# Loads of delta * x written six units ahead instead of seven, later planned landings, and two tiles in turn, in a four-layer scan, edge and attention kernel

## The chip, the cores and the metric

The kernel runs on one core of one Trainium2 chip. The metric is the device time of one execution in microseconds (us), as the median of three runs. An execution agrees with the others to within 2.3 us (14132.37 to 14134.62).

## The reference, cut to what matters

The input x has shape (4, 64, 64, 128): four images of 4096 places with 128 channels. Four layers follow each other. Layers 0 and 1 hold a selective scan, and they are where the change lies. Layer 2 gates nine neighbours of each place; layer 3 is attention over 7 x 7 neighbourhoods. Both run after the scans and are not touched.

Layer 0 splits the channels in two halves of 64. The left half passes two 3 x 3 convolutions; the right half is projected to 128 channels, passes a 3 x 3 depthwise convolution and the scan. Layer 1 normalizes its input, projects it to 256 channels twice (one half is convolved depthwise and scanned, the other is a gate), and adds a two-layer perceptron afterwards. In both, the scan goes over the 4096 places in four directions k (rows, columns, and both backwards), for each channel d and 16 states n:

```
delta = softplus(dt)                           # dt, B, C: projections of x
h[d,n] = exp(delta[d] * A[d,n]) * h[d,n] + (delta[d] * x[d]) * B[n]
y[d]   = sum over n of h[d,n] * C[n]
```

The four directions' y are added, with a skip term D * x.

## The kernel before, in words

**The scans.** A task is 128 channels of one image: 4 tasks in layer 0, 8 in layer 1 (two per image). A task has 16 steps, which are 4 directions by 4 pieces of 1024 places. A step has 16 units; a unit is 8 channels by 16 states on the 128 partitions, over 1024 places. So there are 12 x 16 x 16 = 3072 units. `Scans.run` (from line 556) is a loop over units u. In slot u it writes out, for each engine, work of several units:

- SP (SyncE) issues all transfers. `load(u + 7)` (lines 614 and 615, body from 422) brings delta * x of one unit from DRAM into a tile dub of 512 KB, repeated over the 16 states. Dub has five buffers (line 427), so a load waits until POOL has read the load five before. What it reads, dud, is written per step by one transfer at line 394. The first load of a step (g == 0) first flushes all waiting transfers of the preparation (lines 424 and 425).
- POOL (GpSimd) multiplies dub by B for unit u + 3 (`times_b`, line 436) into one half of a pair tile h, of which there are three.
- PE (TensorE) spreads delta over partitions for unit u + 2 (line 444), from a tile dp that twelve transfers of 64 KB bring per step (line 405), and ACT (ScalarE) takes exp of delta * A (line 446, tile da).
- DVE (VectorE) runs the scan of unit u (line 455) and, for each pair of units, multiplies h by C (line 465). PE then adds over the states (line 536) and ACT copies results and end states (lines 476, 482, 546).

**Preparation and side work.** Beside this loop two lanes of other work are dealt out in small pieces. The lane "prep" (`prepare`, from 317) makes one step's delta, dud, dp and the repeated B and C: it projects x on PE, copies the result to xd (ACT), stores xd to DRAM (`store_xd`, lines 346 to 351), and goes on from there. It starts 22 units before its step, in slots u with (u + 22) % 16 == 0 (lines 582 to 595); in that same slot the last step's leftovers are flushed ("prep" and "rep", line 586). The lane "side" runs the other parts of layers 0 and 1 for other images: `pre0` (projections before the scan, 888), `depthwise` (778), `convs` (925) with `conv` (815), `post0` (955), `pre1` (1000: norm and projection of layer 1), `post1` (1035). These lanes yield, after each piece, the engine that their next piece needs, and may add a time before which it should not be written.

**What sets the order.** No scheduler moves instructions. `Plan` (line 114) keeps an estimate of when each engine is done, in us, with a unit counted as UNIT = 3.6. `Lane.fits` (182) lets a piece be written into the current slot if the estimate says that it is done in time. Three constants say how long after its issue a transfer is taken to have landed: LANDING (8.0 us, most transfers, line 109), FOUR_LANDING (12.0, four loads at once in `post1`, line 110), ROWS_LANDING (17.0, the padded rows of the convolutions, line 111). They are used when a lane waits for a load (`fetch` 740, `halves` 766, `prepare` 320 and 356) and when a tile that is being stored should be free again (`store` 712, `when` 724). Stores and preparation transfers are not issued where they are written: `post` (137) puts them in a list with the estimated time of their data, and `flush` (144) issues those that are due at the beginning of a slot. So between two dub loads on SP stands the group of transfers that became due, or were written directly, in one slot.

**Tiles of the side lane.** `Side.tile` (695) has one buffer each for the tags d0, d1, sq, o and x2 (128 x 512, 256 KB), and two for x and pad. In `pre1` (lines 1018 to 1024) the two projections m = 0 and 1 of a chunk go through sq to DRAM (xid), and the norm of the next chunk writes sq again (line 863). In `convs` (936 to 947) each result of the first convolution goes through d0 to DRAM (ld); `conv` yields a plain "ACT" for it (line 839), with no regard to the store before. ACT's write into such a tile waits until the earlier store has read it. Instructions written through `Counted` (74) all carry line 97.

Of the kernel before, what the change touches and what calls it, by code (L numbers as in the profile page):

```python
# [18 lines left out]
H = 64  # L19
# [86 lines left out]
UNIT = 3.6  # L106
USUAL = dict(PE=1.4, ACT=0.7, TAB=3.3, POOL=1.3)
SLACK = dict(PE=1.2, ACT=2.2, POOL=3.0)
LANDING = 8.0
FOUR_LANDING = 12.0  # L110
ROWS_LANDING = 17.0


class Plan:
# [154 lines left out]
class Scans:  # L269
# [286 lines left out]
    def run(self, between):  # L556

        total = NU * len(self.tasks)
        first = self.tasks[0]
        first.W.load()  # L560
        for _ in self.fetch(first):
            pass
        for _ in self.prepare(first, 0):
            pass
        self.plan.start()
        pieces, fetch, fetched = Lane(self.plan, "prep", iter(())), iter(()), 0
        for u in range(-7, total):
            if u >= 0:
                self.scan(u)
            if 0 <= u + 3 < total:  # L570
                self.times_b(u + 3)
            if u >= 0 and u % NG == 0:
                self.bring_c(u)
            if u > 0 and u % 2 == 0:
                self.save(u // 2 - 1)
            if 0 <= u + 2 < total:
                self.decay(u + 2)
            if u > 0 and u % 2 == 0:
                self.add_up(u // 2 - 1)
            if u > 0 and u % 8 == 0:  # L580
                self.keep(u - 1)
            if u > 0 and u % 8 == 1:
                self.sum_so_far(u - 1)
            even, eighth, first_one = u % 2 == 0, u % 8 == 1, u % NG == 0
            self.plan.slot(
                u, 1.6 * even + 1.0 * eighth, 0.25 * even + 0.7 * (u % 8 == 0) + 1.1 * first_one
            )
            ahead, rest = divmod(u + AHEAD, NG)
            if rest == 0:
                while pieces.step():  # L590
                    pass
                self.plan.flush("prep", "rep")
            if rest == 0 and 0 < ahead < total // NG:
                n, step = divmod(ahead, NU // NG)
                if step == 0 and self.tasks[n].W is not self.tasks[n - 1].W:
                    self.tasks[n].W.load()
                if step == 0 and fetched < n:
                    fetch, fetched = self.fetch(self.tasks[n]), n
                    for _ in range(self.tasks[n].W.nct):
                        next(fetch, None)  # L600
                pieces = Lane(self.plan, "prep", self.prepare(self.tasks[n], step))

            n, step = divmod(ahead + 1, NU // NG)
            if step == 0 and fetched < n < len(self.tasks) and self.tasks[n - 1].x_done:
                fetch, fetched = self.fetch(self.tasks[n]), n
            next(fetch, None)
            while (pieces.count < rest - 4 or pieces.fits()) and pieces.step():
                pass
            if u >= 0:
                n, i = divmod(u, NU)  # L610
                if self.later:
                    self.later.pop(0)()
                between(n, i)
            if 0 <= u + 7 < total:
                self.load(u + 7)
        self.add_up(total // 2 - 1)
        self.save(total // 2 - 1)
        self.keep(total - 1)
        while self.later:
            self.later.pop(0)()  # L620


class Side:
# [191 lines left out]
    def conv(self, w, src):  # L815


        lo, hi = slice(0, H), slice(H, P)
        yield "SP"
        self.flush()  # L820

        def load(pad, half):
            self.rows(pad, hi, src, half * HW // 2 - 1, HW // 2 + 2)
            self.rows(pad, lo, src, half * HW // 2, HW // 2)

        tiles, start = self.halves(load)
        for c in range(0, NCH, 2):
            if c % 4 == 0:
                pad, landed = tiles.pop()
                if c == 0:  # L830
                    start(1)
            yield "PE", landed
            ps = self.bank()
            for t, (dy, dx) in enumerate(((0, 1), (0, 0), (0, 2), (2, 0), (2, 1), (2, 2))):
                part = hi if dy else slice(0, P)
                for j, half in enumerate((lo, hi)):
                    row = (c % 4 + j) * ROWS + dy
                    self.tap(ps[half, :], w[part, dx + 3 * (dy > 0), :], pad[part], row, dx, start=t == 0, stop=t == 5)
                yield "PE" if t < 5 else "ACT"
            yield c, ps  # L840

    def centered(self, xs, i):
# [45 lines left out]
    def pre0(self, b):  # L888

        self.before = True  # L890
        nc = self.nc
        wt = self.weights(self.d0a[:, 0 : 3 * P])
        cv12, inp = wt[:, 0:P], wt[0:H, P : 3 * P]
        lo, hi = slice(0, H), slice(H, P)
        x = self.fetch("x", self.x0[b, :, chunk(0)])
        for c in range(NCH):
            yield ("PE", self.landed) if c == 0 else "PE"
            ps = self.bank()
            nc.tensor.matmul(ps, cv12, x, start=True, stop=True)
            if c + 1 < NCH:  # L900
                x = self.fetch("x", self.x0[b, :, chunk(c + 1)])
            yield self.when("TAB", "d0")

            rl = self.tile("d0")
            self.act(rl, ps, AF.Silu, scale=self.cv12g, bias=self.cv12b)
            yield "PE POOL"
            l = self.tile("sq")
            nc.gpsimd.tensor_scalar(l[hi], rl[hi], self.bn0g[hi], self.bn0b[hi], ALU.mult, ALU.add)
            ps = self.bank()
            nc.tensor.matmul(ps, inp[:, 0:P], rl[lo], start=True, stop=True)  # L910
            yield self.when("ACT", "d1")
            xi = self.tile("d1")
            nc.scalar.copy(xi, ps)
            self.store("d1", self.xid[0, b, 0][:, chunk(c)], xi)
            self.store("sq", self.ld[b][0][:, chunk(c)], l[hi])
            yield "PE"
            ps = self.bank()
            nc.tensor.matmul(ps, inp[:, P : 2 * P], rl[lo], start=True, stop=True)
            yield self.when("TAB", "o")
            sz = self.tile("o")  # L920
            self.act(sz, ps, AF.Silu)
            self.store("o", self.szd[0, b, 0][:, chunk(c)], sz)
        yield from self.depthwise(self.dww0, self.dwb0, self.xid[0, b, 0], self.xcd[0, b, 0])

    def convs(self, b):

        self.before = True
        nc = self.nc
        yield "SP"
        wt = self.weights(self.d0a[:, 3 * P :])  # L930
        c3, cw = wt[:, 0:H], wt[:, H:].rearrange("p (n t c) -> p n t c", n=2, t=6)
        lo, hi = slice(0, H), slice(H, P)
        for i in range(2):
            for item in self.conv(cw[:, i], self.ld[b][i]):
                if isinstance(item, str) or isinstance(item[0], str):
                    yield item
                    continue
                c, ps = item
                l = self.tile("d0")
                nc.scalar.activation(l, ps, AF.Relu, scale=self.bn12g[i], bias=self.cb[:, i : i + 1])  # L940
                if i == 0:
                    self.store("d0", self.across(self.ld[b][1], 0, H, c), l)
                    yield "PE"
                    continue
                yield "PE"
                ps = self.bank()
                for half in (lo, hi):
                    nc.tensor.matmul(ps[half, :], c3[half], l[half], start=True, stop=True)
                yield self.when("ACT", "o")
                o = self.tile("o")  # L950
                nc.scalar.activation(o, ps, AF.Relu, bias=self.c3b)
                self.store("o", self.across(self.catd[b], 0, H, c), o)
                yield "PE"

    def post0(self, b):
# [3 lines left out]
        wt = self.weights(self.d0b)  # L959
        cv, outp, cv3 = wt[lo, 0:H], wt[:, H : 2 * H], wt[:, P : 2 * P]  # L960
        y = self.fetch("x", self.yd[0, b, 0][:, chunk(0)])
        yield "PE", self.landed
        for c in range(NCH):
            ns = []
            sz = self.tile("x2")
# [34 lines left out]
    def pre1(self, b):  # L1000
# [1 line left out]
        nc = self.nc  # L1002
        inp = self.weights(self.w1a)
        x = self.fetch("x", self.x1[b, :, chunk(0)])
        yield "PE", self.landed

        def project(m, xn):
            ps = self.bank()
# [3 lines left out]
        for c in range(NCH):  # L1012
# [4 lines left out]
                x = self.fetch("x", self.x1[b, :, chunk(c + 1)])  # L1017
            for m in range(2):
                ps = project(m, xn)
                yield self.when("ACT", "sq")  # L1020
                xi = self.tile("sq")
                nc.scalar.activation(xi, ps, AF.Identity, bias=self.bias1[:, m : m + 1])
                self.store("sq", self.xid[1, b, m][:, chunk(c)], xi)
                yield "PE"
            for m in range(2, 4):
                ps = project(m, xn)
# [1005 lines left out]
```

## Time and profile before

| what | value |
|---|---|
| median of 3 runs | 14134.09 us |
| lowest and highest run | 14132.37, 14134.62 us |
| profiled execution, its own time | 14152.81 us |
| its span, first to last instruction | 14151.0 us |
| DVE busy | 12084.3 us (85%) |
| PE, POOL, ACT busy | 10247.9 (72%), 9862.8 (70%), 8111.5 us (57%) |
| DMA: share of 16 engines, bytes | 73.3%, 2559.53 MB |
| granted TensorE clock, mean | 0.737 |
| scans: first dub load issued, last one read | 193.3 us, 11474.0 us |
| one scan of a unit (line 455), one product with C for two units (line 465), one product with B (line 436) | 2339, 2288, 2357 ns |

How to read it: the scans fill the first four fifths of the span, layers 2 and 3 the rest. DVE, PE, ACT and POOL execute; SP only issues transfers ("SPq") and is never counted busy. A waits row "A L1 <- B L2: total, times, longest" gives idle time of engine A just before instructions of its line L1, put down to what ended it: an instruction of engine B, or, after "DMA", the landing of a transfer "to<-from". For SP it is the time from its last instruction to the release of the next. A timeline row gives the start, the length, the engine, the line, the operation, the tiles, the number of merged instructions, and in brackets the idle time before it.

### The profile page before, as it was taken

The page shows a single profiled execution, that of the slowest core. Times are in us where ns is not written, and L with a number is a line of the kernel's source. Part 1 is how long each engine was busy: PE and PEld are TensorE (multiplying, and loading weights), DVE is VectorE, ACT ScalarE, POOL GpSimd, SP SyncE. Part 2 cuts the span into 40 slices and gives each one's busy share as a digit, 9 for nine tenths or more (in the row PEclk, how much of TensorE's full clock was granted, in tenths as well). Part 3 has the DMA queues.
Part 4 walks back from the last instruction along what each step waited for, and adds up shares of the span by engine and source line. Part 5 has one row for each costly group of instructions (what it writes and reads, how often), then busy time and mean ns, then how long its engine had stood idle before and what let it go on. Part 6 is the DMA issues. An engine that isn't in the chain of part 4 may idle for free. (4 is left out here: it accounts for less than half of the span.)

```text
span 14151.0 us, 120242 instructions
## 1 busy us (share of the span) xinstructions
PE 10247.9 (72%) x36408; PEld 2607.7 (18%) x36408; DVE 12084.3 (85%) x6647; ACT 8111.5 (57%) x10782; POOL 9862.8 (70%) x4606
## 2 busy tenths in 40 slices
PE   5777777777766777677776777777776766657999
PEld 1111111111111111111111111111111111113555
DVE  4899899989998899889998999999999945775666
ACT  3666566655665566556665555555555556654555
POOL 4777788778877788778887888888888853550000
PEclk7666767777677766677667777767777768878999
DMA  6888888888889888988889888888888842442000
GB/s 163 217 217 226 211 215 224 212 222 209 218 220 209 209 215 208 219 205 219 220 213 223 221 205 210 203 204 218 201 207 201 202 113 68 102 107 66 13 14 8
DMA packets 900351, 2567.23 MB, mean 181 GB/s; under 512 B 145271, under 2 KB 166911, under 8 KB 891511
## 3 DMA queue, kind: packets, MB, share of 16 engines
q1 hardware_dynamic: 899703, 2559.53, 73.3%
q8 instruction: 291, 4.77, 0.2%
q14 instruction: 357, 2.92, 0.1%
HBM read 2135.67 MB, written 272.37 MB: 170 GB/s over the span
## 5 line engine op out<-in xcount | busy, mean ns | idle before, releaser
L436 POOL TENSOR_TENSOR h<-dub,repB 128x1024 f32<-128x1024 f32 x3072 | 7173.7, 2357 | 1146.2 <-DMA dub<-dud 771.1
L455 DVE TENSOR_TENSOR_SCAN h<-da,state,h 128x1024 f32<-128x1024 f32 x2304 | 5324.0, 2339 | 492.2 <-ACT da L446 236.6
L446 ACT ACTIVATE da<-da,av 128x1024 f32<-128x1024 f32 x3072 | 3338.5, 1088 | 2906.8 <-PE da L444 2887.5
L444 PE MATMUL da<-dp,spread 96*128 96x512 bf16 x6144 | 2529.8, 505 | 2399.8 <-DVE h L455 2329.0
L465 DVE TENSOR_TENSOR hc<-h,C 128x2048 f32<-128x2048 f32 x1536 | 3513.6, 2288 | 139.4 <-ACT C L482 80.3
L536 PE MATMUL yps<-hc,gather 128*32 128x512 f32 x12288 | 2470.9, 889 | 5.6 <-DVE hc L465 5.6
L455 DVE TENSOR_TENSOR_SCAN h<-da,h 128x1024 f32<-128x1024 f32 x768 | 1729.7, 2279 | 373.3 <-POOL h L436 283.7
L444 PEld LDWEIGHTS <-spread 96*128 96x128 bf16 x6144 | 563.3, 108 | 5697.2 <-issue 5518.7
L97 POOL TENSOR_TENSOR delta<-delta,low 128x1024 f32<-128x1024 f32 x192 | 452.0, 2354 | 768.0 <-ACT low L97 648.3
L97 PE MATMUL ms<-d,wts 128*128 128x512 f32 (+3 forms) x900 | 691.5, 891 | 237.4 <-POOL d L97 119.9
L97 ACT ACT_TABLE_LOAD x600 | 769.8, 1283 | 12.4 <-PE ms L97 1.8
L97 PE MATMUL ms<-xd,xpdt 8*128 8x512 f32 (+1 forms) x768 | 630.2, 912 | 130.8 <-ACT xd L97 38.0
L97 ACT CAST parts<-delta 128x1024 bf16<-128x1024 f32 x384 | 400.6, 1043 | 363.2 <-POOL delta L97 348.9
L519 PE MATMUL yps<-y,ident 128*128 128x512 f32 x576 | 506.4, 969 | 94.9 <-ACT y L546 94.3
L97 ACT ACTIVATE low<-ms,av 128x512 f32<-128x512 f32 x384 | 263.9, 687 | 529.5 <-PE ms L97 523.9
L97 PE MATMUL ms<-pad,diag 96*32 96x504 f32 (+1 forms) x2304 | 404.6, 809 | 180.9 <-DMA pad<-xid 155.1
L1811 ACT ACTIVATE s<-s,nmax 128x512 f32<-128x512 f32 x512 | 366.1, 717 | 249.9 <-DVE nmax L1808 245.0
L97 POOL TENSOR_TENSOR low<-delta,xc 128x1024 f32<-128x1024 f32 x192 | 501.9, 2614 | 1.6
L1439 ACT ACTIVATE hid<-hid,relb 128x1024 f32<-128x1024 f32 x288 | 323.0, 1146 | 258.5 <-DVE hid L1434 258.4
L536 PEld LDWEIGHTS yps<-hc,gather 128*32 128x32 f32 x12288 | 283.8, 128 | 1012.7 <-issue 1004.5
L1541 POOL TENSOR_TENSOR acc<-acc,part 128x1024 f32<-128x1024 f32 x120 | 314.2, 2625 | 213.3 <-DVE part L1535 158.8
L1800 PE MATMUL sps<-k,q 32*128 32x512 f32 x1024 | 440.7, 658 | 21.2 <-DVE s L1807 21.2
(275 smaller groups left out, 11286.6 us busy)
## 6 DMA issues: line engine op xcount, KB each, us to landing
dub<-dud SPq DMA_DIRECT2D x3072, 512.0 KB
dp<-parts SPq DMA_DIRECT2D x2304, 64.0 KB
repB<-xdd SPq DMA_DIRECT2D x192, 512.0 KB
repC<-xdd SPq DMA_DIRECT2D x192, 512.0 KB
dud<-low SPq DMA_DIRECT2D x192, 512.0 KB
spread<-gd SPq DMA_DIRECT2D x72, 1024.0 KB
pad<-xid SPq DMA_DIRECT2D x192, 256.0 KB
szd<-o SPq DMA_DIRECT2D x96, 256.0 KB
```

The source lines that it names most:

```text
L97: return call(*args, **kw)
L436: self.nc.gpsimd.tensor_mul(dbu, self.live.pop(("dub", u)), t.prepared[step]["B"])
L444: self.nc.tensor.matmul(da[:, cols], self.C.spread[:, jj, :], dp[:, j, cols], start=True, stop=True)
L446: self.nc.scalar.activation(da, da, AF.Exp, scale=t.W.a[:, at : at + 1])
L455: nc.vector.tensor_tensor_scan(h[:, way], da[:, way], h[:, way], 0.0 if step % NSTEP == 0 else t.states[step - 1][:, u % NG : u % NG + 1], ...
L465: nc.vector.tensor_mul(hc, pair, t.prepared[step]["C"].unsqueeze(1).to_broadcast([P, 2, TS]))
L519: self.nc.tensor.matmul(self.like_part(yps, k), self.C.ident, self.part(t.y, k, c, b), start=True, stop=False)
L536: self.nc.tensor.matmul(out, self.C.gather[jj], rhs, start=False, stop=jj == 3)
L1439: nc.scalar.activation(hid, hid, AF.Gelu, bias=self.relb[:, m, t : t + 1])
L1541: (nc.vector if alone and pair else nc.gpsimd).tensor_add(acc, acc, part)
L1800: nc.tensor.matmul(sps[:, h, :], q[ch, toks], k[ch, keys], start=True, stop=True)
L1811: nc.scalar.activation(s[:, i, :], s[:, i, :], AF.Exp, bias=nmax[:, h : h + 1], accum_out=total[:, h : h + 1],)
```

## The change

Four things are changed; the computation stays the same.

- The loop writes `load(u + 6)` at the end of slot u instead of `load(u + 7)`. The buffers of dub stay five.
- LANDING goes from 8 to 10, FOUR_LANDING from 12 to 14, ROWS_LANDING from 17 to 18.
- In `pre0`, `post0` and `pre1` the wait for the first load of the stage is planned with FOUR_LANDING from now on instead of LANDING from the load.
- In `pre1` the two projections go through d1 and sq in turn instead of sq twice. In the first and second convolution the result goes through d0 and d1 in turn instead of d0 always, and the piece that writes it is planned no sooner than its tile is taken to be free.

```diff
--- before.py
+++ after.py
@@ -106,9 +106,9 @@
 UNIT = 3.6
 USUAL = dict(PE=1.4, ACT=0.7, TAB=3.3, POOL=1.3)
 SLACK = dict(PE=1.2, ACT=2.2, POOL=3.0)
-LANDING = 8.0
-FOUR_LANDING = 12.0
-ROWS_LANDING = 17.0
+LANDING = 10.0
+FOUR_LANDING = 14.0
+ROWS_LANDING = 18.0
 
 
 class Plan:
@@ -611,8 +611,8 @@
                 if self.later:
                     self.later.pop(0)()
                 between(n, i)
-            if 0 <= u + 7 < total:
-                self.load(u + 7)
+            if 0 <= u + 6 < total:
+                self.load(u + 6)
         self.add_up(total // 2 - 1)
         self.save(total // 2 - 1)
         self.keep(total - 1)
@@ -836,7 +836,7 @@
                 for j, half in enumerate((lo, hi)):
                     row = (c % 4 + j) * ROWS + dy
                     self.tap(ps[half, :], w[part, dx + 3 * (dy > 0), :], pad[part], row, dx, start=t == 0, stop=t == 5)
-                yield "PE" if t < 5 else "ACT"
+                yield "PE" if t < 5 else self.when("ACT", f"d{c // 2 % 2}")
             yield c, ps
 
     def centered(self, xs, i):
@@ -894,7 +894,7 @@
         lo, hi = slice(0, H), slice(H, P)
         x = self.fetch("x", self.x0[b, :, chunk(0)])
         for c in range(NCH):
-            yield ("PE", self.landed) if c == 0 else "PE"
+            yield ("PE", self.nc.now + FOUR_LANDING) if c == 0 else "PE"
             ps = self.bank()
             nc.tensor.matmul(ps, cv12, x, start=True, stop=True)
             if c + 1 < NCH:
@@ -936,10 +936,11 @@
                     yield item
                     continue
                 c, ps = item
-                l = self.tile("d0")
+                tag = f"d{c // 2 % 2}"
+                l = self.tile(tag)
                 nc.scalar.activation(l, ps, AF.Relu, scale=self.bn12g[i], bias=self.cb[:, i : i + 1])
                 if i == 0:
-                    self.store("d0", self.across(self.ld[b][1], 0, H, c), l)
+                    self.store(tag, self.across(self.ld[b][1], 0, H, c), l)
                     yield "PE"
                     continue
                 yield "PE"
@@ -959,7 +960,7 @@
         wt = self.weights(self.d0b)
         cv, outp, cv3 = wt[lo, 0:H], wt[:, H : 2 * H], wt[:, P : 2 * P]
         y = self.fetch("x", self.yd[0, b, 0][:, chunk(0)])
-        yield "PE", self.landed
+        yield "PE", self.nc.now + FOUR_LANDING
         for c in range(NCH):
             ns = []
             sz = self.tile("x2")
@@ -1002,7 +1003,7 @@
         nc = self.nc
         inp = self.weights(self.w1a)
         x = self.fetch("x", self.x1[b, :, chunk(0)])
-        yield "PE", self.landed
+        yield "PE", self.nc.now + FOUR_LANDING
 
         def project(m, xn):
             ps = self.bank()
@@ -1017,10 +1018,11 @@
                 x = self.fetch("x", self.x1[b, :, chunk(c + 1)])
             for m in range(2):
                 ps = project(m, xn)
-                yield self.when("ACT", "sq")
-                xi = self.tile("sq")
+                tag = ("d1", "sq")[m]
+                yield self.when("ACT", tag)
+                xi = self.tile(tag)
                 nc.scalar.activation(xi, ps, AF.Identity, bias=self.bias1[:, m : m + 1])
-                self.store("sq", self.xid[1, b, m][:, chunk(c)], xi)
+                self.store(tag, self.xid[1, b, m][:, chunk(c)], xi)
                 yield "PE"
             for m in range(2, 4):
                 ps = project(m, xn)
```

In the changed kernel the lines from 940 on stand one lower, those of `pre1` from about line 1021 on two lower.

## The prediction

> **What bounds the kernel now.** Three stretches of the profiled run come first: units 16 to 1023 (layer 0's scans), 1024 to 2047 and 2048 to 3071 (layer 1's), busy time by engine.
>
> ```profile
> 259.00:4028.00 3769.00, 2760.25 (x8696) 543.46 (x8696) 3433.40 (x1514) 2307.27 (x2794) 3016.14 (x1398) 0.69 0.88 217
> 4033.00:7866.00 3833.00, 2708.97 (x8950) 544.79 (x8951) 3487.52 (x1538) 2253.74 (x2753) 3060.14 (x1415) 0.71 0.88 215
> 7871.00:11485.00 3614.00, 2580.45 (x7787) 579.07 (x7785) 3476.78 (x1540) 2048.78 (x2615) 3140.54 (x1436) 0.72 0.84 205
> ```
>
> After the length come PE, PEld, DVE, ACT, POOL, then clock, DMA share and GB/s. DVE sets the pace: 0.91, 0.91 and 0.96 busy, about 3.42 us of work a unit against 3.67 us of time. It idles 336, 345 and 137 us. The last stretch runs the same scans beside little side work (no convolutions, no projections). So some 400 us of idle time come with the side work, and nothing that this change moves can be worth more.
>
> Next, who DVE waits for (from 240 to 11485 us), and behind them POOL, PE and ACT:
>
> ```profile
> DVE h L455 <- ACT da L446: 305.4, 297, 10.2
> DVE h L455 <- POOL h L436: 289.4, 156, 11.8
> DVE hc L465 <- ACT C L482: 80.3, 67, 4.5
> DVE h L455 <- ACT state L476: 76.7, 56, 12.6
> POOL h L436 <- DMA dub<-dud: 760.0, 319, 18.8
> PE ms L97 <- DMA pad<-xid: 128.6, 25, 10.3
> ACT sq L97 <- DMA xid<-sq: 57.3, 18, 13.8
> ACT d L97 <- DMA ld<-d: 33.0, 4, 9.6
> ```
>
> Each row gives total, times, longest. These are two kinds of late transfer: the 512 KB loads of delta * x (dub), which hold POOL and then DVE; and side transfers, which hold PE or ACT, so that the next decay (da) is late.
>
> SP issues every transfer in order. Its own waits in the same stretch:
>
> ```profile
> SPq L429 <- POOL h L436: 4183.5, 1735, 13.3
> SPq L429 <- DMA dud<-low: 277.2, 40, 12.9
> SPq L348 <- ACT xd L97: 172.2, 49, 9.5
> ```
>
> In 1735 of 3072 loads SP stands at line 429 until POOL has read the load five before, since there are five buffers. Whatever is written behind such a load waits as well. One start of a step (16 units) shows the jam; first SP, then POOL:
>
> ```profile
> 4303.72 0.34 SPq L394 DMA_DIRECT2D dud<-low  x1
> 4317.00 0.53 SPq L429 DMA_DIRECT2D dub<-dud  x1
> 4317.58 7.60 SPq L405 DMA_DIRECT2D dp<-parts  x12
> 4325.23 1.87 SPq L429 DMA_DIRECT2D dub<-dud  x3
> ```
>
> ```profile
> 4311.15 2.12 POOL L97 TENSOR_TENSOR parts<-delta,parts 128x1024 bf16<-128x1024 f32 x1
> 4321.65 2.35 POOL L436 TENSOR_TENSOR h<-dub,repB 128x1024 f32<-128x1024 f32 x1 [3.70 <-DMA dub<-dud]
> 4329.83 2.35 POOL L436 TENSOR_TENSOR h<-dub,repB 128x1024 f32<-128x1024 f32 x1 [5.82 <-DMA dub<-dud]
> 4333.61 4.67 POOL L436 TENSOR_TENSOR h<-dub,repB 128x1024 f32<-128x1024 f32 x2 [1.24 <-DMA dub<-dud]
> ```
>
> The step's first load cannot leave before dud has landed, 13.3 us after its store. Only then do twelve dp loads (7.60 us of issue) go, though their data were ready at 4313.27, and only then the second unit's load. An unhindered load is read 4.6 us after its issue (4325.23 to 4329.83).
>
> **The change, part by part.** Both programs have the same number of instructions; no work is added or removed. The sum is made against the profiled run, 14152.8 us (span 14151.0 and 1.8 around it); the median of the runs is 14134.1, 18.7 lower, and the gain is taken off that.
>
> *Loads six ahead.* In SP's order each group of other transfers changes places with the dub load before it. The buffers stay five, so a load still can't leave before POOL frees one: where SP waits there now, the load leaves when it left. What stands behind it leaves up to one unit (3.67 us) sooner.
>
> A row first, then a rule against this part: the median dub load is issued 0.0 us after its buffer is free and read 13.7 us after its issue (counted over all loads). The Trainium skill, "DMA: Bandwidth & Descriptors", section "Rules for kernel authors", says to issue a DMA early and to wait for it late. By that rule every load written a unit later loses cover, term 5 below would stand at its bound of 100, and the sum would be a gain of 40; by the row more than half of the loads lose nothing, and term 5 stays at 20.
>
> Term 1, the start of a step. In the program's order 54 of 191 steps have all twelve dp loads just ahead of the step's first load, where 56 had them behind it. In the step shown, dp would start at 4313.3 and end at 4320.9; the first load leaves then, the second at 4321.5. POOL starts the two units at 4325.5 and 4327.9 instead of 4321.65 and 4329.83, and the waits of 1.24 and later should go: 10.8 us of waits become about 7.5. Counted by place in the step, second units hold 218 us of POOL's 760 in 75 waits, and DVE waits 69 us for POOL there; half is 34. The dp loads themselves come sooner: PE's sequencer and PE wait 78 us for dp in 40 places, with 73 us of DVE idle within 9 us behind them; half is 37. Term 1: 70, bounds 0 and 142.
>
> Term 2, side loads (pads, x, xd). PE waits 229 us for them in 39 places, mean 5.9 (pad from xid 128.6, xd 27.8, pad from ld 26.8, x from yd 23.3, x from the input 22.5). Posts and stores that pads read leave up to 3.67 us sooner, and the plan puts the reader 1 us (pads), 2 us (others) or 6 us (first load of a stage) later. Short waits can't lose more than they are; I take 160 of 229. Behind these waits DVE idles 187 us in all, partly the same idle time as that of dub; I take 40% of 160. Term 2: 65, bounds 0 and 187. Planning later costs nothing while the side work keeps up, and in the changed program's order it stands some eight units sooner on the mean, not later.
>
> Term 3, two tiles in turn. ACT's 57.3 and 33.0 us are writes into sq and d0 while the last store still reads them. With two tiles and a planned wait for the right one, these go; DVE idles 42 us behind them. Term 3: 40, bounds 20 and 42. Late next there is PE's projection, as in any other piece.
>
> Term 4, a loss. Line 425 flushes the waiting preparation transfers ahead of a step's first dub load. One slot later, that flush also takes the next step's store of xd, which ACT has hardly been given: in the program's order this holds in 33 of layer 0's 64 steps, in none before. SP then waits for ACT's copy with the first dub load behind it, and all later ones. Counted in the trace, that copy ends 2.3 us (median) before POOL starts the step's first unit now. Two stores (1.3) and an unhindered load (4.6) after it make POOL some 3.6 us late; summed with the late copies, 238 us in 33 steps. POOL's product is ready 7 us (median) before DVE needs it there; beyond that lead 83 remain, some of them in steps whose second load is late today as well. I take 35, bounds 0 and 238.
>
> Term 5, a loss. Other groups wait for their producers (stores, xdd, rep); a dub load that must be there one unit sooner now stands behind them. SP waits over 2 us in 338 groups, yet only some 30 of POOL's 760 us go back to such waits, since 13.7 - 4.6 = 9 us of cover absorb most. With 3.67 us less cover I take 20, bounds 0 and 100.
>
> Sum: 70 + 65 + 40 - 35 - 20 = 120. 14152.8 - 120 = 14032.8 for a run like the profiled one, or **14014** on the median's scale.
>
> **The rivals.**
>
> *The margins open (gain over 200).* SP's jams cause most of POOL's 760 us. If they clear, idle time in the first two stretches falls by two thirds of the way to the last one's: 400 x 2/3 = 267, 13867. For it: waits feed each other (a late dub load delays the pads behind it, which delay PE). Against it: the ACT and C waits at step starts are ACT's own load.
>
> *Nothing moves (within 0.2%).* DMA is 0.88 busy in the two stretches. If landing is set by that queue and not by issue, terms 1 and 2 vanish: 40 - 55 = -15, 14149. Against it: the second load of the step shown waited 16.3 us for its issue and 4.6 us for its data.
>
> *Slower: xd's store blocks SP.* Term 4 at its full 238 instead of the 35, once POOL's lead over DVE (7 us at a first unit, but a median of 2.3 at layer 0's second units) is used up in the step before: 175 - 238 = -63, 14197. It decides from about 5 us of POOL delay in each of those 33 steps, which the lead can't win back.
>
> **Chances.** Forecast (gain of 28 to 200) 0.50; margins open 0.18; nothing moves 0.11; slower 0.21. Faster by over 0.2% (28 us, about what a measurement can tell from no change) 0.68, within 0.11, slower 0.21. Range 13870 to 14180: down to the open margins, up to most of the slower case.
>
> **What would show it.** Right: dp loads ahead of a step's first dub load; POOL's wait for dub well under 760; ACT's waits for xid and ld gone; PE's wait for pad under 60; idle time of the first two stretches near 270 each, and the third hardly changed. Wrong: SP's wait for ACT's xd far over 172 with POOL's wait for dub at first units of layer 0 up (term 4); pad waits unchanged (term 2). If POOL waits more for dub than now, the rule on early issue was right and the sum fails.

## The result, and the profile after

The changed kernel takes 14123.92 us (median of 12 runs, 14105.99 to 14148.53). The kernel before takes 14132.88 us beside it (12 runs, 14122.38 to 14146.19). The ratio is 0.9998, with a 95% interval of 0.999 to 1.0007: no difference that can be measured. (Over twelve runs the kernel before spreads over 24 us, ten times what its first three runs showed.) The profiled execution took 14143.9 us, its span is 14142.1 us, the mean granted clock 0.734.

First the same three stretches of time in the changed kernel, busy time by engine, columns as before:

```profile
259.00:4028.00 3769.00, 2751.61 (x8697) 544.18 (x8694) 3424.89 (x1510) 2315.42 (x2806) 3014.80 (x1398) 0.69 0.89 217
4033.00:7866.00 3833.00, 2743.59 (x9036) 545.34 (x9035) 3525.15 (x1557) 2268.11 (x2773) 3094.06 (x1430) 0.71 0.89 217
7871.00:11485.00 3614.00, 2568.03 (x7712) 575.44 (x7709) 3446.33 (x1525) 2025.01 (x2586) 3105.18 (x1419) 0.72 0.84 203
```

DVE idles 344, 308 and 168 us (length less the third busy time) where it idled 336, 345 and 137. I had named 270 each for the first two and a third hardly changed as the signs of being right. The windows are those of the kernel before, and the changed kernel is some 37 us ahead when the third begins; by its own units (16 to 1023, 1024 to 2047, 2048 to 3071) DVE idles 344, 306 and 153 us, and the stretches take 3781.0, 3794.6 and 3633.8 us instead of 3773.5, 3838.4 and 3618.3. So in this one execution of each kernel 44 us were won in the second stretch, and most of it was lost again: 7 in the first, 16 in the third, 13 behind the scans.

Then the waits of DVE, POOL and PE of the changed kernel, from 240 to 11485 us:

```profile
DVE h L455 <- POOL h L436: 350.1, 174, 14.8
DVE h L455 <- ACT da L446: 257.7, 280, 11.7
DVE h L455 <- ACT state L476: 36.2, 36, 2.8
POOL h L436 <- DMA dub<-dud: 936.5, 375, 17.2
PE ms L97 <- DMA pad<-xid: 19.6, 7, 3.9
```

Here the reader sees an exchange. The side waits went, more thoroughly than I had forecast: pad from xid 128.6 to 19.6, ACT's waits for xid and ld (57.3 and 33.0) no longer among the rows. With them DVE waits 48 us less for da and 40 less for ACT's state. But POOL waits 176 us more for dub (760.0 to 936.5), and DVE 61 more for POOL (289.4 to 350.1); its waits for C rose by 12. The sum is -16, and the medians differ by -9. (Rows come from one execution each. Both executions profiled here are some 20 us above their medians; differences of that size are not read further.)

SP's waits of the changed kernel, same window, tell what the loads stand behind now:

```profile
SPq L429 <- POOL h L436: 3215.4, 1518, 12.8
SPq L348 <- ACT xd L97: 352.2, 71, 11.8
SPq L405 <- POOL parts L97: 318.9, 163, 8.3
SPq L394 <- POOL low L97: 247.2, 139, 6.9
```

SP waits less for a free buffer (4183.5 before) and more for producers: for ACT's xd 352 instead of 172, for POOL's parts 319 instead of 36 (of the lesser rows of before, `SPq L405 <- POOL parts L97: 36.1, 67, 4.8`). In the same window, all waits other than those of line 429 rose from 1715 to 2981 us, and SP's waits as a whole hardly moved (6854 and 6891). The wait for dud's landing (277.2 before) is down to 3.3; the time in which SP stood there is now taken up by the dp loads.

One step start shows how. SP in the kernel before, at layer 0's unit 128:

```profile
661.28 0.51 SPq L429 DMA_DIRECT2D dub<-dud  x1
661.89 8.16 SPq L405 DMA_DIRECT2D dp<-parts  x12
670.09 0.59 SPq L429 DMA_DIRECT2D dub<-dud  x1
```

The same place in the changed kernel, SP, and then POOL:

```profile
651.72 16.83 SPq L405 DMA_DIRECT2D dp<-parts  x12
668.60 0.59 SPq L429 DMA_DIRECT2D dub<-dud  x1
```

```profile
659.25 2.14 POOL L97 TENSOR_TENSOR parts<-delta,parts 128x1024 bf16<-128x1024 f32 x1
673.41 2.35 POOL L436 TENSOR_TENSOR h<-dub,repB 128x1024 f32<-128x1024 f32 x1 [4.76 <-DMA dub<-dud]
679.19 2.34 POOL L436 TENSOR_TENSOR h<-dub,repB 128x1024 f32<-128x1024 f32 x1 [3.42 <-DMA dub<-dud]
683.56 2.37 POOL L436 TENSOR_TENSOR h<-dub,repB 128x1024 f32<-128x1024 f32 x1 [2.02 <-DMA dub<-dud]
```

The twelve dp loads now start ten microseconds sooner, and take 16.83 us instead of 8.16, since the third of them stands until POOL has made its parts (659.25 + 2.14 = 661.39; that load leaves at 661.41). The step's first load, whose buffer POOL had freed at 656.7, leaves only at 668.60. In the kernel before it left 10.3 us after dud's store (651.01); the same from the store here (648.67) would be about 659. So the first load leaves at 668.60 instead of 661.28, and the second no sooner, at 670.79 instead of 670.09. POOL's three waits there were 4.44, 3.50 and 1.89 us at units 129 to 131; they are now 4.76, 3.42 and 2.02 us at units 128 to 130. The jam was not cleared but shifted by one unit.

Counted over all steps, POOL's waits for dub are these (times, us):

| place in the step | before | after |
|---|---|---|
| first unit | 28, 53 | 92, 303 |
| second unit | 75, 218 | 33, 69 |
| third to fifth | 61, 154 | 39, 107 |
| all others | 155, 335 | 211, 457 |

First and second units together went from 271 to 372 us.

In 54 of the 191 steps that follow the first one, all twelve dp loads now stand between the step's first dub load and the dub load before it. From the first of them to the end of the last they take 14.3 us at the median (7.7 to 20.9); in the kernel before, where 56 steps had the twelve behind the first load, it was 8.2. In 49 of the 54 one of them waits for its parts; 162 of SP's 319 us for POOL's parts are these. At the first and second units of these 54 steps POOL waited 18 and 118 us for dub in the kernel before, and waits 195 and 26 now.

PE got its dp sooner. Its waits for dp, before and then after, on the sequencer (PEld) and in PE:

```profile
PEld L444 <- DMA dp<-parts: 50.0, 28, 4.8
PE da L444 <- DMA dp<-parts: 27.7, 12, 3.9
```

```profile
PEld L444 <- DMA dp<-parts: 14.1, 13, 1.7
PE da L444 <- DMA dp<-parts: 26.4, 9, 4.0
```

### The profile page after: what moved, and what is told of

The parts are those of the page before. It is cut to its first block, busy times and chain, and to the rows that moved or that the text cites. A ratio compares the mean times of both kernels' runs of the same rounds, so it can differ in the third digit from the quotient of the medians.

```text
span 14142.1 us, 120207 instructions
## 1 busy us (share of the span) xinstructions
PE 10269.8 (73%) x36408; PEld 2614.3 (18%) x36408; DVE 12076.7 (85%) x6647; ACT 8107.1 (57%) x10782; POOL 9862.3 (70%) x4606
## 5 line engine op out<-in xcount | busy, mean ns | idle before, releaser
L97 POOL TENSOR_TENSOR delta<-delta,low 128x1024 f32<-128x1024 f32 x192 | 451.8, 2353 | 593.5 <-ACT low L97 539.0
L97 PE MATMUL ms<-d,wts 128*128 128x512 f32 (+3 forms) x900 | 675.2, 876 | 198.7 <-POOL d L97 101.7
L97 PE MATMUL ms<-xd,xpdt 8*128 8x512 f32 (+1 forms) x768 | 631.1, 913 | 127.2 <-ACT xd L97 34.9
L97 ACT CAST parts<-delta 128x1024 bf16<-128x1024 f32 x384 | 400.9, 1044 | 399.5 <-POOL delta L97 375.0
L97 ACT ACTIVATE low<-ms,av 128x512 f32<-128x512 f32 x384 | 263.9, 687 | 525.2 <-PE ms L97 506.7
L97 POOL TENSOR_TENSOR low<-delta,xc 128x1024 f32<-128x1024 f32 x192 | 501.8, 2614 | 1.5
L97 PE MATMUL ms<-pad,diag 96*32 96x504 f32 (+1 forms) x2304 | 410.9, 818 | 94.0 <-DMA pad<-xid 48.2
```

Source lines behind the costliest of these rows:

```text
L97: return call(*args, **kw)
```

## The experiments

After the first comparison three theories stood against each other for the place where the gain of tiles and landings goes. One: the dp loads, now ahead of a step's first load (term 1 with the wrong sign). Two: the store of xd, flushed early (term 4). Three: the general rotation, every load one slot later behind every other group (term 5). A fourth possibility was that landings and tiles bring nothing by themselves. In the texts recorded ahead of the runs, the first four (six_alone to undo_six) call it theory 1 that the parts cancel and theory 2 that nothing here is on the path; from no_flush to late_posts theory A is the store of xd, B the dp loads and C the rotation.

The table gives all runs; "us" is the ratio less one, times 14130, known to 12 to 19 us either way (5 to 12 timed runs each; the kernel before, beside them, has medians of 14126 to 14133). Two runs are told apart here where their intervals do not overlap.

| run | what it is | median us | ratio to before, 95% | us |
|---|---|---|---|---|
| six_alone | before, six ahead | 14122.39 | 0.9995 (0.9987 to 1.0004) | -7 |
| land_alone | before, new landings | 14123.95 | 0.9993 (0.9984 to 1.0002) | -10 |
| tiles_alone | before, two tiles | 14087.88 | 0.9976 (0.9965 to 0.9986) | -34 |
| undo_six | landings and tiles, seven ahead | 14081.23 | 0.9967 (0.9955 to 0.9979) | -47 |
| six_tiles | after, old landings | 14118.62 | 0.9988 (0.9979 to 0.9997) | -17 |
| six_land | after, old tiles | 14171.49 | 1.0029 (1.0018 to 1.0039) | +41 |
| after | all | 14123.92 | 0.9998 (0.999 to 1.0007) | -3 |
| no_flush | after, xd's store on its due time | 14106.97 | 0.9991 (0.9982 to 1.0) | -13 |
| first_seven | after, a step's first load seven ahead | 14080.27 | 0.9973 (0.9963 to 0.9984) | -38 |
| first_six | undo_six, a step's first load six ahead, no flush | 14110.77 | 0.9989 (0.998 to 0.9997) | -16 |
| start_alone | before, a step's first load six ahead, no flush | 14132.97 | 1.0002 (0.9994 to 1.0011) | +3 |
| rot_only | before, all other loads six ahead | 14126.12 | 0.9999 (0.999 to 1.0007) | -1 |
| late_posts | after, posts one slot later | 14137.47 | 1.0011 (1.0002 to 1.0019) | +16 |
| burst_second | undo_six, dp behind the second load | 14072.67 | 0.9956 (0.9944 to 0.9969) | -62 |
| burst_spread | undo_six, dp four to a slot | 14019.44 | 0.9923 (0.991 to 0.9937) | -109 |
| six_spread | after, dp four to a slot | 14036.91 | 0.9937 (0.9925 to 0.9949) | -89 |
| spread_alone | before, dp four to a slot | 14067.03 | 0.9956 (0.9943 to 0.9968) | -62 |

### The parts alone

**six_alone**: the kernel before with the loads six ahead.

```diff
-            if 0 <= u + 7 < total:
-                self.load(u + 7)
+            if 0 <= u + 6 < total:
+                self.load(u + 6)
```

> The kernel before with the loads written six units ahead and nothing else. Theory 1 (two sides cancel): the order on SP costs what the other parts gain; POOL's wait for dub rises from 760 to over 900 us, SP's wait for ACT's xd from 172 to over 300, and the time is 14160 to 14230 (ratio 1.002 to 1.007). Theory 2 (nothing of this is on the path, idle time only moves to another wait): within 0.2%, 14106 to 14162.

Measured: no difference (-7). POOL waits 908.3 us for dub, DVE 383.0 for POOL (94 more) and 216.5 for da (89 less); PE's wait for pad from xid halves to 62.7. The exchange seen in the whole change is this part's own, but the loss that theory 1 expected with it did not come.

**land_alone**: the kernel before with the new constants and stage starts.

```diff
-LANDING = 8.0
+LANDING = 10.0
-            yield ("PE", self.landed) if c == 0 else "PE"
+            yield ("PE", self.nc.now + FOUR_LANDING) if c == 0 else "PE"
...
```

> The kernel before with the later planned landings and nothing else; loads stay seven ahead. Theory 1: PE's waits for pad, x and xd fall from 229 to under 120 us and the time to 14070 to 14110 (ratio 0.995 to 0.998). Theory 2: the same waits fall, the time stays within 0.2%, 14106 to 14162.

Measured: -10, not told from nothing. The waits of DVE and PE in this run:

```profile
DVE h L455 <- ACT da L446: 313.4, 313, 10.7
DVE h L455 <- POOL h L436: 278.1, 140, 15.0
PE ms L97 <- DMA pad<-xid: 85.5, 19, 8.6
```

Pads, x and xd hold PE for 166 us in all instead of 229 (85.5 + 46.7 + 32.7 + 0.7), more than the 120 I wanted; DVE's wait for da does not fall at all (305.4 before), its wait for ACT's state does (76.7 to 34.8). Taking these waits from PE did not bring the decay sooner.

**tiles_alone**: the kernel before with two tiles in turn.

```diff
-                l = self.tile("d0")
+                tag = f"d{c // 2 % 2}"
+                l = self.tile(tag)
...
-                yield self.when("ACT", "sq")
+                tag = ("d1", "sq")[m]
+                yield self.when("ACT", tag)
```

> The kernel before with the two tiles in turn and nothing else. Both theories: ACT's waits for xid and ld (90 us) go. Theory 1: 14080 to 14110, about the 42 us of DVE idle time counted behind them. Theory 2: within 0.2%, 14106 to 14162.

Measured: -34. ACT's waits for xid and ld are gone, DVE's for POOL fell by 40 to 249.8. The waits that term 3 names went, and the time is the size it gave.

**undo_six**: the changed kernel with the loads seven ahead again.

```diff
-            if 0 <= u + 6 < total:
-                self.load(u + 6)
+            if 0 <= u + 7 < total:
+                self.load(u + 7)
```

> The changed kernel with the loads written seven ahead again: landings and tiles stay. Theory 1: POOL's wait for dub back to about 760 us, and what the other parts gain stands alone, 14030 to 14090 (ratio 0.993 to 0.997). Theory 2: within 0.2%, 14106 to 14162.

Measured: -47. One row of POOL's waits, then one of SP's:

```profile
POOL h L436 <- DMA dub<-dud: 746.5, 297, 18.6
```

```profile
SPq L405 <- POOL parts L97: 54.6, 84, 5.1
```

Both are back near the kernel before (760.0 and 36.1). What tiles and landings bring (-34 and -10 by themselves, -47 together) is whole without the six-ahead loads, which cost 44 on top of it. So the fourth possibility falls, and the loss lies in this one line. (This kernel's profiled execution, 14102.73 us, is 21 above its median, so only large differences of its rows to those of other runs are read below.)

### Which of the loads

**no_flush**: the changed kernel without lines 424 and 425, so that xd's store leaves when it is due (the lines below stand two lower there).

```diff
-        if g == 0:
-            self.plan.flush("prep")
```

> The changed kernel without the flush of waiting preparation transfers ahead of a step's first dub load; the next step's xd store then keeps its own due time (in 33 of 64 steps of layer 0). Changed 14124, with seven ahead again 14081. Theory A (term 4, xd's store blocks SP): 14080 to 14105. Theory B (the twelve dp loads ahead of the first load) and theory C (every group's wait for its producer now has a dub load behind it): 14112 to 14136.

Measured: -13, 10 better than the changed kernel by ratio and 17 by the medians, with intervals that overlap, and between the ranges of the theories. SP still waits 292.0 us for ACT's xd. The store accounts for a small part at most, if any.

**first_seven**: the changed kernel, only each step's first load seven ahead.

```diff
-            if 0 <= u + 6 < total:
+            if 0 <= u + 6 < total and (u + 6) % NG:
                 self.load(u + 6)
+            if 0 <= u + 7 < total and (u + 7) % NG == 0:
+                self.load(u + 7)
```

> The changed kernel with only each step's first dub load seven slots ahead again, so that the dp loads stand behind it and no xd store ahead of it; all others six ahead. Theory A and theory B: 14075 to 14105. Theory C: 14112 to 14136.

Measured: -38, which is undo_six's -47 within the error: one load in sixteen holds the loss, with whatever changes places with it. Its waits:

```profile
DVE h L455 <- POOL h L436: 291.1, 141, 13.2
DVE h L455 <- ACT da L446: 251.9, 279, 11.8
POOL h L436 <- DMA dub<-dud: 821.0, 336, 18.5
```

POOL's waits at first units fell from 303 to 8 us, and rose at second units from 69 to 264. Against undo_six DVE waits 33 us more for POOL and 66 less for da, and the time is no better: on the other fifteen loads the exchange brings nothing.

**first_six**, the converse: undo_six, with only a step's first load six ahead, and no flush.

```diff
-            if 0 <= u + 7 < total:
+            if 0 <= u + 6 < total and (u + 6) % NG == 0:
+                self.load(u + 6)
+            if 0 <= u + 7 < total and (u + 7) % NG:
                 self.load(u + 7)
```

> The changed kernel with all loads seven ahead but each step's first six ahead, and without the flush: against seven ahead throughout (14081), only the dp loads change places with the first load. Theory B: 14100 to 14130, POOL's waits for dub at first units up from about 54 to over 200 us. Theories A and C: 14065 to 14095. Term 1 as predicted: 14040 to 14070.

Measured: -16, 31 worse than undo_six. First and second units hold 307 and 7 us of POOL's waits, 313 together, where undo_six has 54 and 207, 262. SP's wait for parts rises from 54.6 to 163.0. So about 30 of the loss of 44 come with the step's first load behind the dp loads (and whatever else is issued in that slot). That the rest is the store of xd fits no_flush, but lies within the error.

**start_alone**: the same edit in the kernel before, without the flush here too.

```diff
-            if 0 <= u + 7 < total:
+            if 0 <= u + 6 < total and (u + 6) % NG == 0:
+                self.load(u + 6)
+            if 0 <= u + 7 < total and (u + 7) % NG:
                 self.load(u + 7)
```

> The kernel before with each step's first dub load six ahead, behind the dp loads, without the flush; nothing else. If that order costs by itself what it costs beside landings and tiles (30 us): 14145 to 14175. If it is free here, as going six ahead as a whole is (14122): 14110 to 14142.

Measured: +3, no loss. POOL's waits move as in first_six (first units 324 us, second 5), yet DVE waits for POOL 289.8 (289.4 before) and for da 277.2. What costs 31 beside tiles and landings is free without them. This speaks against a fixed price of the place.

**rot_only**: the kernel before, all loads but a step's first six ahead.

```diff
-            if 0 <= u + 7 < total:
+            if 0 <= u + 6 < total and (u + 6) % NG:
+                self.load(u + 6)
+            if 0 <= u + 7 < total and (u + 7) % NG == 0:
                 self.load(u + 7)
```

> The kernel before with six ahead for all loads but each step's first; landings and tiles as before. If going six ahead has a gain of its own (pads, x and dp sooner) that only the step starts eat up: 14085 to 14110 and PE's wait for pad under 80 us. If it has none: 14115 to 14140.

Measured: -1. DVE's wait for da falls by 57 and for the state by 20, its wait for POOL rises by 52; PE's for pad from xid falls from 128.6 to 58.6. Gain and loss of the rotation cancel.

**late_posts**: the changed kernel, with every posted transfer issued one slot later, which gives posts and loads about their old order.

```diff
-            if chain in chains or due <= self.now and chain not in held:
+            if chain in chains or due + UNIT <= self.now and chain not in held:
```

> The changed kernel with every waiting transfer issued one slot (3.6 us of plan) later than it is due, so that outside the starts of steps it stands behind the same dub load as with seven ahead; loads into x, pad and so on stay a slot earlier. Theory C: 14070 to 14100, SP's waits for POOL's low (247 us) and ACT's o (287 us) fall to half. Theory A: 14112 to 14140; theory B the same.

Measured: +16, no better than the changed kernel (the intervals overlap). SP's wait for producers falls (for POOL's low from 247 to 90), and POOL waits 944.8 us for dub all the same. With first_seven and rot_only the third theory falls: the general rotation is not the loss.

### Whether the parts add up

**six_tiles**: the changed kernel with the old landings.

```diff
-LANDING = 10.0
+LANDING = 8.0
-            yield ("PE", self.nc.now + FOUR_LANDING) if c == 0 else "PE"
+            yield ("PE", self.landed) if c == 0 else "PE"
...
```

> The changed kernel with the old landings: six ahead and two tiles. If landings and six ahead relieve the same waits, so that six ahead is free without the landings and costs 43 with them: 14080 to 14100 (as with the tiles alone, 14088). If six ahead costs its 43 beside the tiles as well: 14115 to 14140.

**six_land**: the changed kernel with the old tiles.

```diff
-                l = self.tile(tag)
+                l = self.tile("d0")
...
-                xi = self.tile(tag)
+                xi = self.tile("sq")
...
```

> The changed kernel with the old tiles: six ahead and later landings. Later landings alone gave 14124, six ahead alone 14122. If the landings make six ahead costly (they thin out the same waits of PE): 14140 to 14175. If it takes the tiles: 14100 to 14135.

Measured: -17 and +41. So loads six ahead cost -7 alone, 17 beside the tiles (-34 to -17, which overlap), 51 beside the landings (-10 to +41) and 44 beside both. DVE's wait for POOL is 350 to 385 us in all four kernels with six ahead. Its wait for da falls to 216.5 with six ahead alone, and only to 254 to 261 in the other three. Six ahead and the landings take away the same waits of PE (pad from xid 62.7 and 85.5 singly, 32.1 together), so the second to come may find little left to win while it still costs. That is a reading of the rows, not tested by itself, and how the 51 come about in detail they do not tell.

### The dp loads themselves

If twelve dp loads in one go at a step's start are the jam, moving them must help with either order. Leftover dp loads ("rep") are kept in a list and issued after the slot's dub load, all at once behind the second unit's load (burst_second), or at most four in each slot (burst_spread), both in undo_six.

```diff
-                self.plan.flush("prep", "rep")
+                self.plan.flush("prep")
+                waiting += [p[2] for p in self.plan.posted if p[0] == "rep"]
+                self.plan.posted = [p for p in self.plan.posted if p[0] != "rep"]
...
                 self.load(u + 7)
+            while waiting:
+                waiting.pop(0)()
```

> Seven ahead, landings and tiles as changed (14081), and the leftover dp loads of a step issued behind the second unit's dub load instead of ahead of it. If the dp loads ahead of early dub loads are what costs at the start of a step, POOL's waits for dub at second units fall from 207 to under 120 us and the time to 14045 to 14075. If that wait is covered anyway by other waits at the same place (ACT's da and C): 14070 to 14095.

```diff
+            for issue in waiting[:4]:
+                issue()
+            del waiting[:4]
```

> As the run with the dp loads behind the second load, but at most four of them in a slot, in three slots. First theory: POOL's waits for dub over the first five units fall from 397 us to under 300, 14030 to 14070. Second theory: 14070 to 14095. If dp comes too late for PE, PE's waits for dp rise from 19 to over 100 us and the time above 14100.

Measured: -62 and -109. The first is not told from undo_six's -47; it moves the waits on (second units 48 us, third to fifth 213, against 207 and 135 in undo_six). The second is faster beyond the error and shortens them (49 and 140). SP at unit 128 of burst_spread:

```profile
654.83 1.16 SPq L429 DMA_DIRECT2D dub<-dud  x2
656.08 2.47 SPq L405 DMA_DIRECT2D dp<-parts  x4
663.58 0.56 SPq L429 DMA_DIRECT2D dub<-dud  x1
664.18 2.50 SPq L405 DMA_DIRECT2D dp<-parts  x4
```

The first two loads leave together, and four dp loads stand between the next ones. Waits of this kernel:

```profile
POOL h L436 <- DMA dub<-dud: 572.7, 270, 20.9
DVE h L455 <- ACT da L446: 317.1, 308, 16.3
DVE h L455 <- POOL h L436: 175.7, 93, 12.7
PE da L444 <- DMA dp<-parts: 46.9, 14, 9.5
```

In undo_six, which differs only in the dp loads, DVE waits 258.2 us for POOL, 317.6 for da and 80.3 for C; here it is 83 less for POOL, the same for da and 18 more for C (98.1). An idle row fell with little rising in its place, and the time fell with it. The dp loads, up to three slots later, hold PE for 46.9 us. At 14019.44 us this is the best version found, and it beats both kernels.

**six_spread** and **spread_alone**: the same list and the same four to a slot in the changed kernel and in the kernel before.

```diff
                 self.load(u + 6)
+            for issue in waiting[:4]:
+                issue()
+            del waiting[:4]
```

> The changed kernel with the leftover dp loads taken out from ahead of each step's first dub load: four in a slot, behind that slot's dub load; everything else as changed, xd's early store too. If the place of the dp loads makes the cost of six ahead: POOL's waits for dub at first units from 303 to under 180 us, 14020 to 14070. If the cost lies in other transfers: 14095 to 14130.

> The kernel before with the leftover dp loads spread, four in a slot; seven ahead, old landings and tiles. If the jam at the start of a step is a loss of its own, as with landings and tiles in place (62 us there): 14050 to 14090. If it needs them: 14105 to 14140.

Measured: -89 and -62. Spreading is worth 62 in the kernel before, 62 with tiles and landings (-47 to -109), and 86 in the changed one (-3 to -89). Of the 44 that six ahead costs, 20 are left when the dp loads are spread (-109 to -89), and these intervals overlap; six_spread keeps a wait of 482.4 us for ACT's xd, where burst_spread has 183.1. The second theory may have a share there.

## Why the prediction was wrong

The forecast was 14014, the outcome 14123.92, within the range and without a measurable gain.

- **Term 1 (70 gained) failed, and with its sign.** It took one step and said that dp would start at 4313.3 there, take 7.6 us, and that the first load would leave right after it, so that the second came 3.7 us sooner. That step is not even one of the 54 that have the twelve dp loads just ahead of the first load: in the changed kernel its dp loads leave in three groups of eight, one and three, the last of them ahead of its first load, which leaves at 4319.64 instead of 4317.00. In 49 of the 54, dp, written sooner, is not ready sooner: it waits for its parts, the twelve take 14.3 us instead of 7.6, and the step's first load stands behind them. In the place of a second load that comes sooner there is a first load that comes later: in these steps 136 us of POOL's waits at the first two units became 221 (in all steps 271 became 372), where the term took off half of what DVE waited behind second units. The runs price it at about 30 lost beside tiles and landings, and at nothing in the kernel before. My bounds, 0 to 142, excluded a loss without a reason. The other half of the term, PE's waits for dp, fell as said (78 to 40 us), and no run shows time for it by itself.
- **Term 2 (65) was mis-sized in its last step.** The waits fell from 229 to some 48 us, more than the 160 I took off. That 40% of it would reach DVE did not hold: landings alone give 10 and the rotation alone 1, neither told from nothing, and DVE's idle time turned up behind POOL. A wait row on PE that goes is not yet time.
- **Term 3 (40) was right**: 34 by ratio, 39 by the medians of that run, with ACT's two waits gone.
- **Term 4 (35 lost) was of the right kind, its size open**: 10 to 17 by no_flush, not told from nothing. SP's wait for ACT's xd doubled, as foreseen (172.2 to 352.2), and 33 steps do have that store ahead of their first load; but without the flush 292.0 us of the wait are left.
- **Term 5 (20 lost)**: POOL's waits rose at all other units (335 to 457 us), but first_seven and late_posts show no time for it that can be told from nothing. On the Trainium skill's rule ("DMA: Bandwidth & Descriptors", "Rules for kernel authors", issue early and wait late): POOL did wait more for dub, as I said it would if the rule were right and the sum failed. Yet a slot of lead more or less on fifteen of sixteen loads made no time (-38 against -47); what cost was what stood ahead of the sixteenth.

By the runs the change is -34 for the tiles, about -10 for the landings and +44 for six ahead beside them; that they come out at nothing is a balance of errors, not what the forecast or a rival described. The rival *nothing moves* gave the time (14149, within 0.2% of 14123.92), but not by its mechanism, in which the DMA queue sets the landing and terms 1 and 2 vanish. The side loads did land in time for PE, and the spread runs show that the order of issue alone, with the same transfers, is worth 62 to 86 us.

Two slips of the prediction carry nothing: DVE's work is 3.40 us a unit by the rows shown, not 3.42, and the slower rival's 14197 leaves out the 20 us of term 5.

**Open.** Why the new order at a step's start is free in the kernel before and costs 31 beside tiles and landings; why six ahead costs 44 to 51 beside the landings and nothing alone. One lead: in the profiles, one execution each, layer 0's scans (units 16 to 1023) become 23 us shorter with six ahead alone (3750.3 from 3773.5) and 22 longer beside tiles and landings (3781.0 from 3759.0). A sixth dub buffer, which would take the waits of line 429 away, was not tried.

## What to carry to other kernels

A transfer that is written sooner in an in-order queue is priced by what it waits for itself at its new place, since all behind it waits too; count that over all steps, for the one step that is shown need not be like the others. When a wait row falls, look for the row that rose before calling it time, and be slow to add up two parts that relieve the same wait. A burst of small transfers ahead of a large one that the pace hangs on did best here when dealt out a few to a slot (62 to 86 us in three kernels).

## What was not expected of the hardware

A store of 512 KB (dud) followed by a load of what it wrote holds SP long while the DMA engines are 0.88 busy: 13.3 us in the step that the prediction shows (4303.72 to 4317.00), and 277.2 us in 40 such waits in all. A load of the same size there, which nothing hinders, is read 4.6 us after its issue (4325.23 to 4329.83). It is in the time of this landing that the changed order issues the dp loads.
